# A state-space layer beside a quantized feed-forward on one Trainium2 core: normalization shared with ScalarE, a product two tiles late, parameter loads on another queue, and the last output projection between the scans

## The chip, the core and the metric

The kernel runs on one core of a Trainium2 chip, as one program. The metric is device time in microseconds of a whole execution. Several executions are timed, and one execution is recorded by the profiler.

The engines are named as in the profile: PE is TensorE (matrix products, its weight loads are PEld), DVE is VectorE, ACT is ScalarE, POOL is GpSimd, and SP is the engine that here only starts DMA transfers. Each engine works through its own queue in order. An instruction that has to wait holds everything behind it on its engine. A DMA started by SP or ACT is an instruction of that engine's queue too.

## The reference

The input is x, 8192 tokens of 512 numbers (8 sequences of 1024). Everything is float32.

```python
xn = layernorm(x)                     # mean and variance over the 512, no gain
out = x + mamba(xn) + ffn(xn)

# mamba, DI = 1024 channels, 16 states each
xz = xn @ W_in;  xb, z = split(xz)
xc = silu(causal_conv4(xb) + conv_b)
B, C, dt = split(xc @ W_x);  dt = softplus(dt + dt_bias)      # 16, 16, 1 columns
h_t = h_(t-1) * exp(dt * A) + dt * xc * B                     # A = -exp(A_log)
y = (sum over states of h * C + xc * D) * silu(z)
mamba = y @ W_out

# ffn: every operand is rounded to a 4-bit grid in blocks of 16, each block with its own scale
q = lambda v: grid(v / s) * s,  s = max(abs(block)) / 6
h = silu(q(xn) @ q(w_gate).T) * (q(xn) @ q(w_up).T)           # 1408 columns
ffn = q(h) @ q(w_down).T
```

## The kernel before

The program has four stages.

**Preparation** (`prelude`, class `Job`). There are 52 jobs, each a tile of 128 partitions, most of 1024 numbers: two jobs with the first 512 tokens, twelve with parts of w_gate and w_up, eight with parts of w_down (1024 and 384 numbers in turn), and thirty with the other tokens. A job rounds its tile to the 4-bit grid; a token job also normalizes its tile first. Job 0 and 1, 22 and 23, and so on are pairs of the same chunk of 512 tokens and share their statistics. The steps of a job, with their engines:

- `load` (SP): the tile from DRAM, four buffers.
- `measure` (DVE, L94, L95; ACT, L100): mean and variance for both jobs of a pair, then a square root on ScalarE.
- `deviation` (DVE, L112 to L116): one step of refinement and the reciprocal of the deviation, for both jobs of the pair.
- `normal` (POOL, L124): subtract the mean and multiply, in place, one instruction for each half tile (128 x 512).
- `turn_normal` (PE, ACT, L140): transposes of the normalized tile to PSUM, copies to SBUF, and a store that is issued in the next iteration.
- `scale` (DVE, L154 to L159): the largest absolute value of each block, the scale and its reciprocal, and the tile times the reciprocal. The small values are in PSUM, in the pool whose two buffers later hold the decays of the scans.
- `steps` (ACT, L61, L62): Abs and Exp give the size of the rounding step.
- `round_` (POOL, L167, L168): add that size and subtract it again, which rounds.
- `product` (DVE, L172): times the block's scale.
- `turn_quantized` (PE, ACT, SP): transposes, copies and store of the result.

One iteration of the loop issues parts of several jobs, in the order written there by hand. In iteration i they are: the load of i+3, the stores left by the iteration before, some work of the first scan chunk (its projections, convolution and softplus, one piece for each iteration, `ahead`), `turn_normal(i)`, `deviation(i+1)`, `scale(i)`, `steps(i)`, `normal(i+1)`, `round_(i)`, `measure(i+2)`, `product(i-1)` and `turn_quantized(i-1)`. The order on each engine is the order of issue. Some instructions of the first scans are hoisted into the last third of the loop.

Before that, the constructor starts the loads of the parameters on ScalarE's queue (L239 to L256: W_x, W_out with 2 MB, the convolution weights, three vectors, and A_log in four parts with an Exp behind each, L257).

**Sweep 1 and sweep 2** (`sweep`). The tokens are 16 chunks of 512. Each chunk has 64 pairs of scans: `make_u` (POOL, L638), `make_a` (ACT, L650), the scan itself (DVE, L668), the product with C (DVE, L675, four buffers `hc`), and sums over the states on TensorE (`sum_states`, L685, one group for two pairs). After eight pairs comes a `gate` (DVE, L703, L704), which completes one of the eight slices of y. Other work is put between the pairs: the projections of the next chunk (`ahead`), the output projection of the chunk before (`finish`, L735, and the additions L722), and as `others` the feed-forward (`gate_up` in sweep 1, chunks 0 to 9; `downs` in sweep 2, L894, chunks 10 to 15 of the scans). Side work is paced by planned costs: an estimate of what is left is spread evenly over the slots that are left,

```python
        left = cost + len(now) // per * (29.0 + 64.0 + sums)
        slots = len(now) - TAIL
            credit = min(credit + max(left, 0.0) / max(slots, 1), MOST)
```

where 29 stands for one `finish`, 64 for one `ahead`, and `TAIL` is 12 pairs. The last chunk has no `ahead`.

**End** (in `run`). After the last pair of chunk 15 its sums, its gate and its `finish` are issued: for each of four tiles of 128 tokens eight products of 128x128 by 128x512, which are two instructions each on TensorE, then an addition to what was kept for these tokens, and the store of the output.

Of the kernel before, what the change touches and what calls it, by code (L numbers as in the profile page):

```python
# [17 lines left out]
P = 128  # L18
# [9 lines left out]
T = 512  # L28
# [11 lines left out]
AGAIN = "again"  # L40
TAIL = 12
# [24 lines left out]
class Job:  # L66
# [14 lines left out]
    def measure(self):  # L81

        if not self.pair:
            return
        nc, pp, name = self.nc, self.pp, self.name
        jobs = (self, self.pair)
        n = sum(j.G for j in jobs)
        mv = pp.tile([P, n, 2], F32, tag="mv", name=f"mv_{name}")
        i = 0
        for j in jobs:  # L90
            j.mean, j.at = mv, i
            for g in range(j.G):
                stats = pp.tile([P, 6], F32, tag="stat", name=f"stat_{name}_{i}")
                nc.vector.bn_stats(stats, j.x[:, g * j.W : (g + 1) * j.W])  # L94
                nc.vector.bn_aggr(mv[:, i, :], stats)  # L95
                i += 1
        var = mv[:, :, 1]
        root = pp.tile([P, n], F32, tag="root", name=f"root_{name}")
        rstd = pp.tile([P, n], F32, tag="rstd", name=f"rstd_{name}")
        nc.scalar.activation(root, var, AF.Sqrt, bias=self.net.eps)  # L100
        self.var, self.root, self.r = var, root, rstd
        for j in jobs:
            j.rstd = rstd

    def deviation(self):
        if not self.pair:
            return
        nc, var, root, rstd = self.nc, self.var, self.root, self.r
        n = root.shape[1]

        t = self.net.p_y.tile([P, 2, n], F32, tag="py", name=f"newton_{self.name}")
        nc.vector.reciprocal(t[:, 0, :], root)  # L112
        nc.vector.scalar_tensor_tensor(t[:, 1, :], var, EPS, t[:, 0, :], ALU.add, ALU.mult)
        nc.vector.tensor_tensor(t[:, 1, :], root, t[:, 1, :], ALU.add)
        nc.vector.tensor_scalar(t[:, 1, :], t[:, 1, :], 0.5, None, ALU.mult)
        nc.vector.reciprocal(rstd, t[:, 1, :])  # L116

    def normal(self):
        if self.tokens is None:
            return  # L120
        for g in range(self.G):
            x = self.x[:, g * self.W : (g + 1) * self.W]
            i = self.at + g
            self.nc.gpsimd.tensor_scalar(  # L124
                x, x, self.mean[:, i, 0:1], self.rstd[:, i : i + 1], ALU.subtract, ALU.mult
            )
# [21 lines left out]
    def scale(self):  # L148

        nc = self.nc  # L150
        n = self.K // BLK
        small = self.net.p_a.tile([P, 3, n], F32, tag="ah", name=f"qp_{self.name}")
        top, self.sc, rs = small[:, 0, :], small[:, 1, :], small[:, 2, :]
# [4 lines left out]
        self.v = self.pp.tile([P, self.K], F32, tag="qv", name=f"qv_{self.name}", bufs=3)  # L158
# [19 lines left out]
class Net:  # L178
# [11 lines left out]
    def __init__(self, tc, ctx, x, W_in, conv_w, conv_b, W_x, A_log, D_param, dt_bias, W_out,  # L190
# [46 lines left out]
        nc.vector.memset(self.steep, LEAST)  # L237
        self.Wx = cpool.tile([P, J, self.NS], F32, tag="Wx", name="Wx")
        nc.scalar.dma_start(self.Wx, W_x.rearrange("(j p) n -> p j n", p=P))  # L239
        self.Wout = cpool.tile([P, J, DM], F32, tag="Wout", name="Wout")  # L240
        nc.scalar.dma_start(self.Wout, W_out.rearrange("(j p) m -> p j m", p=P))
        self.cw = cpool.tile([P, J, self.H0 + 1], F32, tag="cw", name="cw")
        nc.scalar.dma_start(self.cw, conv_w.rearrange("(j p) o c -> p j (o c)", p=P))
        vecs = []
        for name, v in (("cb", conv_b), ("dtb", dt_bias), ("Dp", D_param)):
            vt = cpool.tile([P, J], F32, tag=name, name=name)
            nc.scalar.dma_start(vt, v.rearrange("(j p) -> p j", p=P))
# [6 lines left out]
        for s in range(SG):  # L254
            rows = slice(s * D4, (s + 1) * D4)
            nc.scalar.dma_start(A_all[rows], A_log.rearrange("(g d) n -> d g n", d=D4))  # L256
            nc.scalar.activation(  # L257
                self.A[rows],
                A_all[rows].rearrange("d g (q s) -> d g q s", s=SG)[:, :, :, s],
                AF.Exp,  # L260
            )
        nc.vector.tensor_scalar(self.A, self.A, -1.0, -SLOW, ALU.mult, ALU.min)
# [10 lines left out]
        self.Win_v = W_in.rearrange("(k p) n -> p k n", p=P)  # L273
# [41 lines left out]
    def prelude(self, pp):  # L315
# [8 lines left out]
        for i in range(3):  # L324
            part(i, "load")
        part(0, "measure")
# [4 lines left out]
        self.behind = []  # L331
        for i in range(n + 1):
# [13 lines left out]
            part(i, "turn_normal")  # L346
            part(i + 1, "deviation")
            part(i, "scale")
            part(i, "steps")
            part(i + 1, "normal")  # L350
# [5 lines left out]
            part(i - 1, "product")  # L356
            part(i - 1, "turn_quantized")
# [385 lines left out]


# [159 lines left out]
    def run(self):  # L904
# [13 lines left out]
        with ExitStack() as ffn:  # L918
            fp = ffn.enter_context(tc.tile_pool(name="ff", bufs=2))
            with tc.manual_schedule():  # L920
# [3 lines left out]
                self.sweep(pairs, range(SPLIT * per), self.gate_up(fp, range(n)), costs[0])  # L924
        with ExitStack() as ffn:
# [5 lines left out]
            with tc.manual_schedule():  # L931
                self.sweep(
                    pairs, range(SPLIT * per, n * per), self.downs(fp, dT, tiles), costs[1]
                )
                last = self.step[n - 1]
                self.sum_states(last, self.J - 1, NG - 1)
                self.advance()
                self.advance()
                for _ in self.finish(last):
                    self.advance()  # L940
                while self.due:
                    self.advance()
# [5 lines left out]
    def sweep(self, pairs, now, others, cost):  # L948
# [6 lines left out]
        slots = len(now) - TAIL  # L955
        credit = 0.0
        for g in now:
# [54 lines left out]
            if summed and pq < NG - 1:  # L1012
                self.sum_states(self.step[pc], pj, pq)
            self.now += 1
        more = True
# [87 lines left out]
```

## Time and profile before

| | |
|---|---|
| three runs | 5172.91, 5178.5, 5181.34 us (median 5178.5) |
| the profiled execution | 5171.58 us, of which the span of the profile is 5169.7 |
| busy, share of the span | PE 84%, DVE 86%, POOL 78%, ACT 65% |
| preparation | about 0 to 500 us |
| the two sweeps | about 500 to 5135 us, the second from about 3560 |
| end | 5135 to 5169.7 us |

Times in the profile are microseconds from the start of the span. A group of instructions is a line of the source, an engine and an operation with its tiles: its count, busy time and mean duration in ns, then the idle time of the engine just before these instructions and what ended it. A row of the timeline is its start, its duration, engine, line and operation; in brackets stands the idle time before it and the releaser. A wait is a line that waited, an arrow, the line that released it, and the total, the number of times and the longest. A stage's row gives the busy time and the number of instructions of each engine inside it, the granted clock of TensorE as a share of full speed, and the busy share and the rate of the DMA engines.

### The profile page before, as it was taken

How to read it: one execution, taken by the hardware profiler on the slowest of the kernel's cores; microseconds unless marked ns; L12 is line 12 of the kernel's file. 1: busy time of each engine (PE TensorE's matmuls, PEld its weight loads, DVE VectorE, ACT ScalarE, POOL GpSimd, SP SyncE). 2: the span in 40 equal slices, each digit the busy share in tenths (PEclk: the TensorE clock that was granted, in tenths of full speed). 3: DMA queues.
4: the chain of work that ended last, by engine and by line, in shares of the span. 5: the costliest groups of instructions: out<-in, count | busy, mean ns of one | idle time of the engine just before them, and what ended most of it. 6: DMA issues, size and time to landing. Idle time of an engine off the chain costs nothing. (4 is left out here: it accounts for less than half of the span.)

```text
span 5169.7 us, 52154 instructions
## 1 busy us (share of the span) xinstructions
PE 4357.2 (84%) x16324; PEld 2286.0 (44%) x16324; DVE 4463.7 (86%) x4087; ACT 3368.9 (65%) x5037; POOL 4050.4 (78%) x2302
## 2 busy tenths in 40 slices
PE   5535889888898898989898898986999999999975
PEld 2324555554555556455554555551333333333321
DVE  6756888888888988888887898888999999999997
ACT  5655766767667677775767867676656665656543
POOL 5887888878888888887887888887768676767664
PEclk9656999999899999999999999996999999999986
DMA  6665566575656657566575656757686868686852
GB/s 196 198 205 157 143 185 182 155 199 170 180 165 173 192 165 208 143 188 180 162 201 154 191 166 182 200 145 207 178 229 177 239 182 240 175 236 184 228 132 61
DMA packets 582275, 937.45 MB, mean 181 GB/s; under 512 B 53216, under 2 KB 329696, under 8 KB 579824
## 3 DMA queue, kind: packets, MB, share of 16 engines
q1 hardware_dynamic: 571600, 931.61, 64.3%
q10 hardware_dynamic: 10400, 2.52, 0.2%
q8 instruction: 130, 2.13, 0.2%
q14 instruction: 145, 1.19, 0.1%
HBM read 676.76 MB, written 257.20 MB: 181 GB/s over the span
## 5 line engine op out<-in xcount | busy, mean ns | idle before, releaser
L638 POOL TENSOR_TENSOR u<-rep,B 128x1024 f32<-128x1024 f32 x1024 | 2411.3, 2361 | 760.9 <-DVE ah L668 691.6
L650 ACT ACTIVATE ah<-rep,A 128x512 f32<-128x512 f32 x2048 | 1415.8, 692 | 1129.0 <-DVE hc L675 1090.3
L675 DVE TENSOR_TENSOR hc<-ah,C 128x1024 f32<-128x1024 f32 x1024 | 1249.5, 1220 | 77.3 <-PE py L685 35.1
L668 DVE TENSOR_TENSOR_SCAN ah<-ah,state,u 128x1024 f32<-128x1024 f32 x512 | 1199.5, 2343 | 87.0 <-ACT u L656 85.9
L668 DVE TENSOR_TENSOR_SCAN ah<-ah,u 128x1024 f32<-128x1024 f32 x512 | 1169.3, 2284 | 52.3 <-ACT ah L650 46.0
L685 PE MATMUL py<-hc,summed 128*32 128x512 f32 x4096 | 653.5, 635 | 170.9 <-DVE hc L675 119.0
L771 PE MATMUL pu<-wu,xq 128*128 128x256 f32 (+1 forms) x3072 | 693.9, 383 | 101.9 <-ACT hT L824 63.1
L771 PE MATMUL pg<-wg,xq 128*128 128x256 f32 (+1 forms) x3072 | 661.7, 373 | 69.8 <-ACT hT L824 23.3
L771 PEld LDWEIGHTS pu<-wu,xq 128*128 128x128 f32 x3072 | 571.7, 203 | 250.6 <-ACT hT L824 86.7
L894 PE MATMUL pod<-dT,hTr 128*128 128x512 f32 x1408 | 641.7, 606 | 13.3 <-DMA hTr<-hT 9.6
L771 PEld LDWEIGHTS pg<-wg,xq 128*128 128x128 f32 x3072 | 554.0, 195 | 210.3 <-issue 69.5
L498 PE MATMUL pz<-xT,wz 128*128 128x512 f32 x1024 | 506.3, 641 | 69.5 <-ACT h L782 34.8
L437 PE MATMUL px<-xT,wx 128*128 128x512 f32 x1024 | 491.9, 625 | 38.8 <-ACT h L782 21.4
L735 PE MATMUL po<-Wout,y 128*128 128x512 f32 x1024 | 463.8, 604 | 10.7 <-ACT hT L824 4.4
L460 POOL TENSOR_TENSOR xc<-xc,taps 128x509 f32<-128x509 f32 x360 | 413.7, 1149 | 44.3 <-ACT taps L454 25.5
L894 PEld LDWEIGHTS pod<-dT,hTr 128*128 128x128 f32 x1408 | 262.7, 192 | 395.2 <-issue 365.1
L498 PEld LDWEIGHTS pz<-xT,wz 128*128 128x128 f32 x1024 | 204.1, 205 | 338.9 <-issue 232.3
L685 PEld LDWEIGHTS py<-hc,summed 128*32 128x32 f32 x4096 | 91.8, 110 | 564.7 <-DVE hc L675 278.7
L437 PEld LDWEIGHTS px<-xT,wx 128*128 128x128 f32 x1024 | 195.3, 198 | 317.7 <-issue 224.2
L735 PEld LDWEIGHTS po<-Wout,y 128*128 128x128 f32 x1024 | 191.2, 192 | 278.7 <-issue 258.4
L786 DVE TENSOR_TENSOR h<-h,pu 128x512 f32<-128x512 f32 x192 | 121.9, 638 | 179.4 <-PE pu L771 166.3
L650 ACT ACT_TABLE_LOAD x209 | 268.1, 1283 | 3.7
(125 smaller groups left out, 4538.4 us busy)
## 6 DMA issues: line engine op xcount, KB each, us to landing
rep<-ddd SPq DMA_DIRECT2D x512, 512.0 KB, 7.1
ddd<-dd SPq DMA_DIRECT2D x128, 512.0 KB, 3.5
hTr<-hT SPq DMA_DIRECT2D x64, 704.0 KB, 5.8
wg<-gu SPq DMA_DIRECT2D x80, 512.0 KB, 4.9
wu<-gu SPq DMA_DIRECT2D x80, 512.0 KB, 5.9
hT<-hT SPq DMA_DIRECT2D x80, 512.0 KB, 2.9
wx<-in_L_attn_W_in_dram SPq DMA_DIRECT2D x128, 256.0 KB, 3.0
wz<-in_L_attn_W_in_dram SPq DMA_DIRECT2D x128, 256.0 KB, 2.9
```

What stands on the lines that cost most here:

```text
L437: nc.tensor.matmul(px, w[:, k, :], s.xT[:, k, :], start=(k == 0), stop=(k == self.KM - 1))
L460: tt(ca[:, H0 - k :], ca[:, H0 - k :], taps[k][:, : T - H0 + k], ALU.add)
L498: nc.tensor.matmul(b[0], w[:, k, :], s.xT[:, k, :], start=(k == 0), stop=(k == self.KM - 1))
L638: self.nc.gpsimd.tensor_tensor(u, s.reps[j][:, h : h + 2, 1, :], s.B[q].unsqueeze(1).to_broadcast([P, 2, T]), ALU.mult)
L650: nc.scalar.activation(ah[:, i, :], s.reps[j][:, h + i, 0, :], AF.Exp, scale=self.A[:, g, q : q + 1])
L668: nc.vector.tensor_tensor_scan(a, a, u.rearrange("p i t -> p (i t)"), 0.0 if s.first else self.state[:, g, q : q + 1], ALU.mult, ALU.add,)
L675: nc.vector.tensor_tensor(hc, ah, s.C[q].unsqueeze(1).to_broadcast([P, 2, T]), ALU.mult)
L685: nc.tensor.matmul(s.py[i * D4 : (i + 1) * D4, :], self.summed, hcs[i // 2][:, i % 2, :], start=(q == 0), stop=(q == NG - 1),)
L735: nc.tensor.matmul(b[0], s.y[:, j, i * P : (i + 1) * P], self.Wout[:, j, :], start=(j == 0), stop=(j == self.J - 1),)
L771: nc.tensor.matmul(b[0][:, i, :], xq[pair][:, k, i * P : (i + 1) * P], w[:, k, :], start=(k == 0), stop=(k == self.KM - 1),)
L786: nc.vector.tensor_tensor(rows, rows, b[0], ALU.mult)
L894: nc.tensor.matmul(b[0], h[:, k, :], dT[:, k, :], start=(k == 0), stop=(k == self.KF - 1))
```

## The change

Four things are changed.

1. `normal`: the first half of each token tile (the first 128x512) is normalized by ScalarE as an Identity with scale 1/deviation and bias -mean/deviation; GpSimd keeps the second half. `deviation` gets two more small VectorE steps for the bias (`off`).
2. The loop: `product` and `turn_quantized` are those of job i-2, and there is one iteration more. `scale(i)` comes before `deviation(i+1)`, and `normal(i+1)` before `steps(i)`. For the longer lag two jobs share one small tile in PSUM, and `qv` has four buffers.
3. The parameters are loaded by SP, behind the first three tiles (`constants`). The Exps of A_log and the load of W_out follow in iteration 1 (`decays`).
4. Sweep 2 gets a planned cost lower by 64 and ends its side work 7 pairs before the end instead of 12. In the last six pairs `finish_last` puts the first seven of the eight products of tiles 0 to 2 and the first four of tile 3 between the scans; tile 3 uses a buffer of the scans' PSUM pool. After the last gate one product each for three tiles and four for the last remain, each with its addition and store.

The core of the diff:

```diff
 deviation:
         nc.vector.reciprocal(rstd, t[:, 1, :])
+        nc.vector.reciprocal(t[:, 0, :], t[:, 1, :])
+        nc.vector.scalar_tensor_tensor(
+            self.off, self.mean[:, :, 0], -1.0, t[:, 0, :], ALU.mult, ALU.mult
+        )
 normal:
+            if g == 0:
+                self.nc.scalar.activation(
+                    x, x, AF.Identity, bias=self.off[:, i : i + 1], scale=self.rstd[:, i : i + 1]
+                )
+                continue
             self.nc.gpsimd.tensor_scalar(
                 x, x, self.mean[:, i, 0:1], self.rstd[:, i : i + 1], ALU.subtract, ALU.mult
             )
 scale:
-        small = self.net.p_a.tile([P, 3, n], F32, tag="ah", name=f"qp_{self.name}")
+        if not net.small:
+            two = net.p_a.tile([P, 2, 3, P // 2], F32, tag="ah", name=f"qp_{self.name}")
+            net.small = [two[:, i] for i in range(2)]
-        self.v = self.pp.tile([P, self.K], F32, tag="qv", name=f"qv_{self.name}", bufs=3)
+        self.v = self.pp.tile([P, self.K], F32, tag="qv", name=f"qv_{self.name}", bufs=4)
 parameters (constants, called behind the first three loads):
-        nc.scalar.dma_start(...)      # W_x, W_out, conv_w, conv_b, dt_bias, D_param, A_log
+        nc.sync.dma_start(...)        # the same without W_out
+        def decays():
+            nc.sync.dma_start(self.Wout, W_out.rearrange("(j p) m -> p j m", p=P))
+            ...                       # the four Exps of A_log, and A = -exp(A_log)
 prelude:
+        decays = self.constants()
-        for i in range(n + 1):
+        for i in range(n + 2):
             part(i, "turn_normal")
+            part(i, "scale")
             part(i + 1, "deviation")
-            part(i, "scale")
+            part(i + 1, "normal")
             part(i, "steps")
-            part(i + 1, "normal")
+            if i == 1:
+                decays()
             part(i, "round_")
             ...
             part(i + 2, "measure")
-            part(i - 1, "product")
-            part(i - 1, "turn_quantized")
+            part(i - 2, "product")
+            part(i - 2, "turn_quantized")
 sweep (LAST = 6, fp is None in sweep 1; sweep 2 is called with costs[1] - 64.0):
-        slots = len(now) - TAIL
+        slots = len(now) - (TAIL if fp is None else LAST + 1)
+            if fp is not None and g >= len(pairs) - LAST:
+                if ending is None:
+                    while next(others, None) is not None:
+                        assert self.room("other")
+                    ending = self.finish_last(s, fp)
+                if g < len(pairs) - 1:
+                    next(ending)
+        if ending is not None:
+            for _ in range(2):
+                next(ending)
+            self.sum_states(s, self.J - 1, NG - 1)
+            ...                       # the last gate, then the rest of finish_last
+    def finish_last(self, s, fp):
+        ...
+        for i in range(3):
+            banks.append(self.bank([P, self.DM], f"po_{t0 + i}"))
+            matmuls(i, range(4))
+            yield
+            matmuls(i, range(4, J - 1))
+            yield
+        ah = self.p_a.tile([P, 2, T], F32, tag="ah", name=f"po_{t0 + 3}")
+        banks.append([ah[:, 0, :], 3])
+        matmuls(3, range(4))
+        yield
+        for i in range(self.TT):
+            matmuls(i, range(J - 1 if i < 3 else 4, J))
+            nc.vector.tensor_tensor(rs[i], rs[i], banks[i][0], ALU.add)
+            nc.sync.dma_start(self.out[t * P : (t + 1) * P, :], rs[i])
```

## The prediction

> **What bounds the kernel now.** I read the slices of the span first, then busy time by stage, then for each stage the timeline, its waits and its groups, and last the chain that ended last. In the slices I look at the first four columns (129 us each) and the last.
>
> ```profile
> DVE  6756888888888988888887898888999999999997
> ACT  5655766767667677775767867676656665656543
> POOL 5887888878888888887887888887768676767664
> PEclk9656999999899999999999999996999999999986
> ```
>
> The preparation (the first 500 us) is the worst part of VectorE's row. Cut into its stages (us, busy time of PE, PEld, DVE, ACT, POOL, then clock, DMA share, GB/s):
>
> ```profile
> 44.50:106.80 62.30, 43.76 (x132) 21.83 (x132) 51.03 (x77) 38.60 (x51) 38.30 (x18) 0.89 0.63 217
> 106.80:171.30 64.50, 41.15 (x122) 20.03 (x121) 46.46 (x92) 40.55 (x58) 35.38 (x23) 0.81 0.56 184
> ...
> 205.00:345.00 140.00, 54.40 (x239) 44.20 (x239) 99.36 (x191) 101.49 (x130) 135.16 (x69) 0.57 0.63 208
> ...
> 5020.00:5137.00 117.00, 53.50 (x128) 5.45 (x128) 112.56 (x70) 51.46 (x98) 65.87 (x29) 0.50 0.27 63
> ```
>
> The first two are the weight jobs: no engine is full, VectorE is nearest. The third is the token jobs: GpSimd is full (135 of 140). The last is the end of the scans: VectorE full, TensorE at half clock. Start of the run, timeline:
>
> ```profile
> 4.30 7.27 ACTq L247 DMA_DIRECT2D cb<-in_L_attn_conv_b_dram  x1
> ...
> 17.38 1.28 ACT L257 ACT_TABLE_LOAD   x1 [17.38 <-DMA Dp<-in_L_attn_D_param_dram]
> ...
> 21.31 0.30 ACT L100 ACTIVATE root_x<-mv_x,eps 128x4 f32<-128x4 f32 x1
> ...
> 26.92 1.23 DVE L154 TENSOR_REDUCE qp_x<-wt_x 128x64 f32<-128x1024 f32 x1 [3.32 <-POOL wt_x L124]
> ```
>
> ScalarE issues the parameter loads one after another until 17 us, and the first square root stands behind them, although the statistics were ready at 8.96. From 106.8 to 171.3, in the weight jobs, the longest of VectorE's waits (total, times, longest) shows the product one tile behind the rounding:
>
> ```profile
> DVE qv_d L172 <- POOL qv_d L168: 6.8, 3, 4.2
> ```
>
> Groups of the token stage, 205 to 345:
>
> ```profile
> L124 POOL TENSOR_SCALAR wt_x<-wt_x,mv_x,rstd_x 128x512 f32<-128x512 f32 x31 | 64.1, 2076 | 0.0
> L167 POOL TENSOR_TENSOR qv_x<-qv_x,qm_x 128x1024 f32<-128x1024 f32 x15 | 32.0, 2130 | 3.7 <-ACT qm_x L62 3.7
> L168 POOL TENSOR_TENSOR qv_x<-qv_x,qm_x 128x1024 f32<-128x1024 f32 x15 | 31.9, 2128 | 1.2
> ```
>
> GpSimd has hardly any idle time (after the bar), and in the same answer VectorE's L154 waits 31.5 us for the normalization L124. The chain at the end:
>
> ```profile
> 5135.42 1.92 PE py L685 x4
> 5137.35 28.58 PE po L735 x64
> ```
>
> After the last scan 64 matmuls stand bare on the path.
>
> **The change part by part.** The sum is made against the profiled execution, 5171.6 us (span 5169.7); the median of the three runs is 6.9 us higher, and I carry that difference over.
>
> Start. Without parameter loads ahead of it, the square root can run at 9.1. Then 0.30, seven small VectorE steps (five took 0.92, two more of 0.17: 1.25), and GpSimd's half, 2.08 with 0.1 of signalling: the first L154 at 13.0 instead of 26.92, 13.9 earlier. The loads now stand on SP's queue, their issue times there adding to 16 us (0.49, 2.37, 7.27, 3.05, 0.59 and 2.3 for A_log), ahead of the fourth tile's load. That one issues near 19 and lands near 23 (median landing of such a load 3.9); its L154 ran at 43.28, so would be at 29.4: hidden with 6 us to spare. The 2 MB load of W_out now goes out at the second tile; behind it on SP's queue stand the sixth tile's load and the store that the first projection needs. At the 400 GB/s that the DMA showed at 10 us it holds them 5 us, inside the 13.9. Decays: four ACTIVATEs of 0.42 and one VectorE step behind them, under 2 us once. I take 13; bounds 5 (the SP issues take twice as long) and 15.
>
> The Trainium skill (DMA: Bandwidth & Descriptors, "Issuing engines are not separate DMA queues") says that the queue a transfer is started from only matters for the sequencer's time to start it, usually small beside the transfer. Here the 4 KB load of cb held ScalarE's queue for 7.27 us, and the measurement decides; by the page this edit would be worth about nothing and the time 13 us longer.
>
> Weight jobs, 44.5 to 171.3. The product two tiles late no longer waits for the rounding: VectorE's waits for L168 in the two stretches are 1.9, 3.3 and 6.8, 12.0 together. Next is VectorE itself (97.5 busy of 126.8), then its waits for ScalarE's convolution rows, 11.1, which I leave. I take 12; bounds 4 and 20.
>
> Token jobs, 171.3 to 456, 284.7 us for 30 jobs: 30 periods of 8.41 (two L124 of 2.08 and L167, L168 of 2.13), 10.0 of GpSimd's L582, and 19.2 in which VectorE stood (358.9 to 378.1) while the first fetches for the scans held the load queue. Afterwards per job GpSimd has 2.08 + 4.26 = 6.34. ScalarE per pair of jobs: 8 copies 4.28, Abs and Exp 4.42, two new Identities priced by L443, the same form from PSUM (0.77), one root 0.30, two table loads 2.57: 13.1, or 6.55 per job. VectorE per pair: two scalings (L154 to L159, 3.66), two products of 1.20, statistics 3.2, the longer deviation 1.25: 14.2. On ScalarE, Abs and Exp of the tile before are queued behind the Identity that waits for the deviation, and GpSimd's rounding waits for them; with the product two tiles later that has a period to spare. On VectorE the deviation stands one product before the scaling that needs it, and GpSimd's half takes 2.08: 0.95 of wait, so 15.1 per pair or 7.56 per job. VectorE is what is late next. 30 x 7.56 = 227; the four softplus steps now meet a tighter ScalarE (1.33 + 2.57 each, half of it shown: 8); L582 fits into GpSimd's slack; the fetch stall stays, 19. Together 254: 30 saved. Bounds: 5, if ScalarE's order keeps the period at 8.41 (279.5), and 53, if neither the wait nor the softplus shows (7.09 per job and 19).
>
> The extra iteration of the loop holds one product, copies and stores that existed before: nothing. The shared small tile frees both jobs' scales two products later, and VectorE is in order past them by then: nothing.
>
> Sweep 2. The estimate that paces the side work falls by 64, and its slots grow by 5: 3.57 per pair instead of 3.79. TensorE was 0.95 busy from 3750 to 5000, VectorE 0.95, against 0.96 alone at the end, so relief can give at most 1% of 1250, 13 us; the same work filling the free end can cost that much. I take 4; bounds -8 and 13.
>
> End. From the last gate but one (y at 5113.94) to the end of the span are 55.8 us. Afterwards TensorE does sums (1.93), 50 matmuls of 0.43 (25 of the 32 products, two each) with four at 0.85 on the cold clock (the row: about 2 us at half clock from 5137.3), and three sums of 1.06: done at 28.3, later than the last scan's 21.5. Sums wait behind projections in TensorE's queue, but the four hc buffers keep VectorE going. Then gate 1.5, 14 matmuls 6.0, one addition 0.8, the store 3.1: 39.7. Saved 16; bounds 8 (half clock throughout the first ten microseconds and again behind the gate) and 22 (warm throughout).
>
> The Trainium skill (TensorE: Matmul & The Clock Gate, "What's actually happening") speaks against this place: after an idle window of 3.4 us work starts at half clock until a busy one has passed. By the page up to 3.4 us start cold instead of about 2, an estimate of 0.7 us lost.
>
> Sum: 13 + 12 + 30 + 4 + 16 = 75. 5171.6 - 75 = 5096.6 for a profiled run, 5103.5 by the median.
>
> **The rivals.** ScalarE becomes the bound of the token stage: it has the least slack (13.1 of 15.1) and its Abs and Exp now stand behind an Identity that waits for the deviation; the waits L167 <- L62 (3.7) speak for it, the two-tile lag against. The stage then gains 5 instead of 30: 5128.5.
>
> Everything hides better: weights 20, tokens 48, sweep 13, end 18, start 14 = 113: 5065.5. For it speaks that VectorE's rows overlap by 0.1 each; against it, that some wait always comes up.
>
> Slower: the same Identity closes a loop per job instead of being slack: deviation 1.25, Identity 0.77, Abs 1.06, table load 1.28, Exp 1.15, GpSimd 2.08 + 4.26 = 11.85 per job. 30 jobs and 27 are 383, 98 more than now; less the 45 of the other parts, 53 slower: 5231.5. It decides from 10.1 us per job (284.7 + 45 - 27 over 30). For it: between 177 and 207 the period was 9.7 to 9.9 with GpSimd waiting for Exp. Against it: the product no longer asks for the same tile.
>
> That it does not do what it says (scheduling moves the root back behind other work, TensorE stays cold): start and token parts zero, 12 + 4 + 8 gives 5154.5, still faster.
>
> **How the numbers follow.** About 0.2% is what a measurement tells from no change (10 us). Forecast 0.62, with a range of its own from 5085 to 5122; ScalarE-bound 0.19; hides better 0.10; does not do what it says 0.04; slower 0.03; cancelled to within 0.2% 0.02. Faster is 0.62 + 0.19 + 0.10 + 0.04 = 0.95, same 0.02, slower 0.03. The range reaches to the ScalarE case above and halfway to the better one: 5080 to 5134.
>
> **What would show it.** First L154 near 13; no wait of products for rounding; token rounds every 7.6 us with GpSimd near 0.84 busy; 25 projections between the last scans and 14 matmuls after the last gate. Wrong if token rounds stay above 8.2, if the fourth tile's load is waited for, or if VectorE waits for TensorE in the last six pairs.

## The result, and the profile after

The changed kernel takes 5138.04 us (median of four runs, 5133.51 to 5139.24) beside 5176.74 for the kernel before on the same chip: a ratio of 0.9927, with a 95% interval from 0.9913 to 0.994. It is 38.7 us faster. The forecast was 75 us less, or 5103.5; the measured time lies 34.5 us above that and 4 above the top of the stated range. The profiled execution took 5139.24 us, its span is 5137.4.

Lines have moved in the changed file: the first line of the scaling is L168 (L154 before), GpSimd's normalization L135 (L124), ScalarE's new half L131, rounding L181 and L182 (L167, L168), the product L186 (L172), Abs and Exp L62 and L63, copies of transposed tiles L151, convolution rows of the first chunk L508 (ScalarE) and L517 (VectorE), softplus L607 and the product behind it L612, the last projections L784.

In the slices of the page, VectorE's first four columns rise from 6756 to 7767, and GpSimd is no longer near full in the second and third:

```profile
DVE  7767888887888988888887898888999999999998
ACT  5866676857668677775767767676656665665543
POOL 5676888888888888887887888787777776767654
PEclk9657999999999999989999999996999999999999
```

By stage (us, busy time of PE, PEld, DVE, ACT, POOL, clock, DMA share, GB/s; the same pieces of work as the four rows of before, except that the last begins at the last gate but one):

```profile
31.00:93.28 62.28, 41.62 (x131) 21.15 (x130) 50.42 (x76) 38.51 (x51) 38.34 (x19) 0.92 0.64 220
93.28:156.20 62.92, 42.70 (x131) 21.61 (x130) 47.01 (x95) 41.60 (x60) 33.32 (x21) 0.86 0.57 187
190.00:330.00 140.00, 59.25 (x258) 48.99 (x259) 104.30 (x214) 113.39 (x151) 110.73 (x56) 0.55 0.65 213
5096.00:5137.00 41.00, 34.89 (x96) 13.18 (x96) 26.19 (x20) 8.19 (x15) 7.86 (x4) 0.92 0.18 64
```

The weight jobs (rows one and two) take 125.2 us where they took 126.8: hardly less, and still no engine is full. In the token jobs (row three) GpSimd fell from 135 to 111 of 140, but nothing else is full either: VectorE 104, ScalarE 113. So waits, not an engine, set the pace there. In the end (row four) TensorE is now busy.

Start, timeline:

```profile
4.62 3.24 SPq L268 DMA_DIRECT2D cb<-in_L_attn_conv_b_dram  x1
...
7.78 0.30 ACT L102 ACTIVATE root_x<-mv_x,eps 128x4 f32<-128x4 f32 x1 [5.76 <-DVE mv_x L97]
...
11.33 1.23 DVE L168 TENSOR_REDUCE qp_x<-wt_x 128x64 f32<-128x1024 f32 x1 [1.95 <-POOL wt_x L135]
```

The root no longer stands behind parameter loads; the first scaling runs 15.6 us earlier. The load of cb, which held ScalarE's queue for 7.27 us, now holds SP's for 3.24, and all the parameter loads together held SP's queue until 12.19 us.

VectorE's waits in the weight jobs, first after (31 to 156), then the row of before that the prediction told of but did not show (44.5 to 171.3):

```profile
DVE xc L517 <- ACT over L508: 21.5, 6, 6.6
DVE qp_x L168 <- POOL wt_x L135: 1.5, 1, 1.5
```

```profile
DVE xc L487 <- ACT over L478: 11.0, 6, 3.4
```

The 12.0 us in which products waited for rounding are gone, as forecast. But the wait for ScalarE's convolution rows grew by 10.5. The longest of the six places in the timeline:

```profile
33.17 1.21 DVE L186 TENSOR_TENSOR qv_x<-qv_x,qp_x 128x1024 f32<-128x1024 f32 x1
...
36.75 5.51 PE L467 MATMUL px<-xT,wx 128*128 128x512 f32 x8 [4.94 <-DMA wx<-in_L_attn_W_in_dram]
...
42.10 1.04 PE L150 MATMUL ptq_x<-ident,qv_x 128*128 128x128 f32 x8
...
42.74 1.07 ACT L151 COPY stq_x<-ptq_x 128x512 f32<-128x512 f32 x2 [7.15 <-PE ptq_x L150]
...
44.37 0.27 ACT L508 ACTIVATE over<-px,cw 128x3 f32<-128x3 f32 x1
...
44.68 1.53 DVE L517 SCALAR_TENSOR_TENSOR xc<-px,cw,xc 128x509 f32<-128x509 f32 x2 [6.57 <-ACT over L508]
```

The product is done at 34.38. Its transposes stand in TensorE's queue behind a projection (L467), which itself waited for its weights; ScalarE's copies wait for the transposes, and the convolution row stands behind the copies.

Waits in the token jobs after, 156.2 to 434:

```profile
DVE qp_x L168 <- POOL wt_x L135: 41.6, 22, 4.9
...
POOL qv_x L181 <- ACT qm_x L63: 47.6, 19, 4.0
...
ACT stn_x L151 <- DMA xnT<-stn_x: 24.5, 8, 6.0
```

VectorE still waits 41.6 us for GpSimd's half (51.2 before), though GpSimd has time to spare. GpSimd itself now waits 47.6 us for Exp (6.4 before). One place in the timeline shows the chain; in brackets stands the idle time before a row and its releaser:

```profile
299.38 1.33 ACT L607 ACTIVATE dd<-row,dtb 128x512 f32<-128x512 f32 x2
...
304.79 1.15 ACT L63 ACTIVATE qm_x<-qm_x,steep 128x1024 bf16<-128x1024 bf16 x1
...
306.02 2.12 POOL L181 TENSOR_TENSOR qv_x<-qv_x,qm_x 128x1024 f32<-128x1024 f32 x1 [2.43 <-ACT qm_x L63]
308.22 2.14 POOL L182 TENSOR_TENSOR qv_x<-qv_x,qm_x 128x1024 f32<-128x1024 f32 x1
310.31 2.51 POOL L612 TENSOR_TENSOR dd<-dd,xc 128x512 f32<-128x512 f32 x2
312.79 2.09 POOL L135 TENSOR_SCALAR wt_x<-wt_x,mv_x,rstd_x 128x512 f32<-128x512 f32 x1
314.91 1.23 DVE L168 TENSOR_REDUCE qp_x<-wt_x 128x64 f32<-128x1024 f32 x1 [4.92 <-POOL wt_x L135]
```

Softplus (L607) delays Exp on ScalarE; rounding waits for Exp; GpSimd's half of a later tile stands in GpSimd's queue behind that rounding and behind L612; and the scaling of that later tile waits 4.92 us. It is a loop over two tiles: scaling of i, Abs and Exp of i, rounding of i, GpSimd's half of i+2, scaling of i+2. A pair of jobs with neither softplus nor the scans' fetches in it (a quiet pair below) takes 15.64 us near the end of the stage; the others (disturbed pairs) take up to 20.9, and the one with the fetches 38.9.

End, timeline of TensorE:

```profile
5099.09 7.92 PE L784 MATMUL po<-Wout,y 128*128 128x512 f32 x14
...
5107.94 6.28 PE L784 MATMUL po<-Wout,y 128*128 128x512 f32 x14
...
5115.14 9.71 PE L784 MATMUL po<-Wout,y 128*128 128x512 f32 x22
...
5127.45 6.28 PE L784 MATMUL po<-Wout,y 128*128 128x512 f32 x14 [1.60 <-DVE y L734]
```

50 matmuls now run before the last gate (the last scan's own work on VectorE ends at 5118.52, so most of the 22 run behind it) and 14 behind the gate.

### The profile page after: what moved, and what is told of

Its sections match the earlier page's. It is cut to its first block, busy times and chain, and to the rows that moved or that the text cites. A ratio compares the mean times of both kernels' runs of the same rounds, so it can differ in the third digit from the quotient of the medians.

```text
span 5137.4 us, 52165 instructions
## 1 busy us (share of the span) xinstructions
PE 4360.9 (85%) x16324; PEld 2294.4 (45%) x16324; DVE 4468.1 (87%) x4119; ACT 3385.0 (66%) x5068; POOL 3985.9 (78%) x2270
## 5 line engine op out<-in xcount | busy, mean ns | idle before, releaser
L715 PE MATMUL py<-hc,summed 128*32 128x512 f32 x4096 | 631.0, 624 | 136.9 <-DVE hc L705 91.8
L955 PE MATMUL pod<-dT,hTr 128*128 128x512 f32 x1408 | 653.4, 614 | 39.4 <-DMA hTr<-hT 26.9
L467 PE MATMUL px<-xT,wx 128*128 128x512 f32 x1024 | 498.9, 632 | 40.5 <-ACT h L843 21.4
L765 PE MATMUL po<-Wout,y 128*128 128x512 f32 x960 | 438.5, 608 | 12.4 <-ACT hT L885 4.4
L467 PEld LDWEIGHTS px<-xT,wx 128*128 128x128 f32 x1024 | 198.0, 201 | 326.9 <-issue 236.5
L765 PEld LDWEIGHTS po<-Wout,y 128*128 128x128 f32 x960 | 179.9, 193 | 265.5 <-issue 247.5
L847 DVE TENSOR_TENSOR h<-h,pu 128x512 f32<-128x512 f32 x192 | 121.9, 638 | 181.1 <-PE pu L832 149.5
```

The source lines that it names most:

```text
L467: nc.tensor.matmul(px, w[:, k, :], s.xT[:, k, :], start=(k == 0), stop=(k == self.KM - 1))
L715: nc.tensor.matmul(s.py[i * D4 : (i + 1) * D4, :], self.summed, hcs[i // 2][:, i % 2, :], start=(q == 0), stop=(q == NG - 1),)
L765: nc.tensor.matmul(b[0], s.y[:, j, i * P : (i + 1) * P], self.Wout[:, j, :], start=(j == 0), stop=(j == self.J - 1),)
L847: nc.vector.tensor_tensor(rows, rows, b[0], ALU.mult)
L955: nc.tensor.matmul(b[0], h[:, k, :], dT[:, k, :], start=(k == 0), stop=(k == self.KF - 1))
```

## The experiments

Twelve kernels ran, in three comparisons of four, each beside its own runs of the kernel before (5166.18, 5170.74 and 5178.93 us). The table cuts each profiled span at the same events: the start of the third job's scaling; that of job 22's; that of job 51's; the first gate; the first gate of chunk 10; the last gate but one; the end. All in us, each within 0.1 of the trace, so that a row adds up to its span. The runs of one comparison (e1 to e4, e5 to e8, e9 to e12) shared a chip.

| kernel | ratio to before (95%) | start | weights | tokens | to first gate | sweep 1 | chunks 10 to 15 | end |
|---|---|---|---|---|---|---|---|---|
| before | | 38.5 | 132.5 | 280.6 | 72.5 | 3114.1 | 1474.2 | 57.2 |
| after | 0.9927 (0.9913, 0.994) | 25.0 | 129.9 | 268.7 | 73.4 | 3121.4 | 1477.1 | 41.8 |
| e1 preparation alone | 0.9958 (0.9943, 0.9972) | 25.0 | 131.1 | 269.2 | 73.7 | 3114.5 | 1474.3 | 57.2 |
| e2 sweep 2 and end alone | 0.9975 (0.9966, 0.9984) | 38.4 | 132.9 | 280.1 | 72.3 | 3110.4 | 1476.9 | 40.8 |
| e3 lag of one tile | 0.9945 (0.9929, 0.9962) | 26.1 | 131.0 | 268.8 | 74.9 | 3111.0 | 1479.9 | 42.2 |
| e4 rounding later | 0.9915 (0.99, 0.993) | 25.0 | 129.1 | 255.2 | 73.8 | 3114.0 | 1479.4 | 42.4 |
| e5 the change again | 0.9931 (0.9916, 0.9946) | 25.0 | 130.4 | 268.5 | 73.3 | 3114.8 | 1479.7 | 42.3 |
| e6 additions later | 0.9916 (0.9901, 0.9931) | 25.0 | 121.8 | 268.4 | 73.3 | 3111.0 | 1479.4 | 42.2 |
| e7 four buffers | 0.9924 (0.9908, 0.9941) | 25.0 | 131.9 | 264.8 | 70.0 | 3105.3 | 1482.4 | 40.8 |
| e8 planned cost as before | 0.9936 (0.9919, 0.9953) | 24.9 | 129.3 | 268.8 | 73.3 | 3111.2 | 1480.5 | 41.8 |
| e9 GpSimd normalizes all | 0.9959 (0.9944, 0.9974) | 27.0 | 133.3 | 285.0 | 72.1 | 3120.5 | 1470.6 | 42.2 |
| e10 e4, e6, e7 together | 0.9859 (0.9844, 0.9874) | 25.1 | 122.6 | 244.7 | 71.1 | 3123.4 | 1474.0 | 42.3 |
| e11 and fetches spread | 0.9816 (0.9799, 0.9834) | 25.0 | 121.9 | 229.4 | 71.0 | 3128.7 | 1479.3 | 40.8 |
| e12 pacing all as before | 0.992 (0.9905, 0.9935) | 25.0 | 130.1 | 270.0 | 71.9 | 3121.5 | 1477.3 | 41.9 |

**e1_prep: the preparation alone.**

```diff
-                    costs[1] - 64.0, fp,
+                    costs[1], None
                 )
+                last = self.step[n - 1]
...
+                for _ in self.finish(last):
+                    self.advance()
```

> The whole preparation of the change with the sweeps and the end of before. In the profile of the change the first gate of the scans came 27.2 us earlier than before, but at the end of sweep 1 only 19.8 us were left. Theory A: the preparation is worth 27 (half of the 55 that were forecast), and what sweep 1 gave back is drift of the granted clock that another execution need not show: 5147 to 5153 us, first gate again near 497. Theory B: sweep 1 answers to the earlier start and always gives 7 back: 5155 to 5158. By the forecast (13 + 12 + 30): 5122.

Measured: 5145.44 against 5166.18 us, 20.7 us less. Up to the first gate the profile is 25.2 us ahead of before; sweep 1 took 3114.5. Theory A holds: the preparation keeps what it gains.

**e2_end: sweep 2 and the end alone.** The hunks of the change in the sweep, `finish_last` and `run`, on the kernel before.

> The preparation of before with the pacing and the end of the change. Theory A: sweep 2 and end together gain 12 to 13 us, because the feed-forward products that used to be done by 5001 us now run into the last chunk, so that part of the 16 us saved at the end is paid for there: 5163 to 5166 us. By the forecast (4 + 16): 5157. If sweep 1 alone loses 7 us from the other start (theory B of the first kernel), sweep 1 is here as long as before, about 3114 us from the first gate to that of chunk 10.

Measured: 5152.68 us, 13.5 less. The end fell by 16.4, chunks 10 to 15 rose by 2.7: what theory A said, with less given back. Both parts together would be 34.2, about what the change shows on this level (e5: 37.0), so no interaction is seen that is clear of the intervals.

**e3_lag1: the lag undone.**

```diff
-            part(i - 2, "product")
-            part(i - 2, "turn_quantized")
+            part(i - 1, "product")
+            part(i - 1, "turn_quantized")
```

> The change with the product and the transposes of the rounded tile one tile late again. Theory A: the lag is worth next to nothing in the weight jobs, because VectorE's wait for the rounding (12.0 us before) only became a longer wait for ScalarE's convolution rows (11.0 us before, 21.5 in the change): with one tile the waits come back on L186 and go from L517, and the rounds of jobs 2 to 21 span 125 to 128 us as in the change (125.2) and before (126.8). In the quiet token pairs the product would be ready at the moment it is issued (rounding ends at 405.87, product at 405.94), so the pair stays near 15.7; total 5138 to 5148. By the forecast the lag is worth 12 in the weight jobs alone: 5150 or more.

Measured: weights 131.0, tokens 268.8, both as in the change. VectorE's waits in the weight jobs (31 to 156) are those of before again:

```profile
DVE xc L517 <- ACT over L508: 11.5, 5, 3.5
DVE qv_d L186 <- POOL qv_d L182: 7.1, 3, 4.4
DVE qv_u L186 <- POOL qv_u L182: 3.4, 1, 3.4
DVE qv_g L186 <- POOL qv_g L182: 2.1, 1, 2.1
```

12.6 us stand at the product and 11.5 at the convolution, where the change has 0 and 21.5. The lag moves a wait from one line to the other. In this form it is worth nothing, in either stage.

**e4_round_late: rounding one tile later.**

```diff
-            part(i, "round_")
+            part(i - 1, "round_")
```

> The change with GpSimd's rounding one tile later, so that GpSimd normalizes its half of tile i+2 before it rounds tile i. Theory A: the token stage is held by a loop over two tiles: scaling of i, Abs and Exp on ScalarE, rounding of i, GpSimd's half of i+2, scaling of i+2; any delay of ScalarE (softplus, a copy that waits for a store) goes through it to VectorE, which waits 41.6 us for L135. With the rounding one tile later these waits fall below 15, a quiet pair takes 14.2 to 14.6 instead of 15.64, and the token stage loses 20 to 28 us: 5110 to 5120. Theory B: ScalarE itself is too full in the disturbed pairs (18 to 20 us): only the quiet pairs gain, 1 us each for six pairs: 5130 to 5136.

Measured: tokens 255.2, 13.5 less than the change; quiet pairs took 14.78 us (rounds at 373.30 and 388.08) instead of 15.64. VectorE's waits from 190 to 320:

```profile
DVE qp_x L168 <- ACT wt_x L131: 10.2, 7, 2.9
...
DVE qp_x L168 <- POOL wt_x L135: 2.6, 3, 0.9
```

In the corresponding stretch of the change (190 to 330) the wait for L135 was 27.9. So the loop over two tiles is the mechanism. Theory A's 20 to 28 was too much: what ScalarE loses in the disturbed pairs now reaches VectorE through ScalarE's own half (L131). With the rounding one tile late, a product one tile late would stand right behind its own rounding; the edit was made with the product two tiles late only, and without that lag it was not run.

**e5_again: the change once more.**

> The changed kernel once more, beside the others of this comparison. Theory A (sweep 1 drifts from execution to execution): sweep 1, from the first gate to that of chunk 10, takes 3110 to 3116 us instead of the 3121.4 of the first profile; first gate near 497 to 500 again; sweep 2 and the end 1518 to 1522. The time is 0.9927 of before again, 37 to 40 us less.

Measured: 5133.78 us, 37.0 less; sweep 1 took 3114.8 with the same code that showed 3121.4. As theory A said, the first profile's 7 us there belong to that execution and not to the code.

**e6_adds_late: the convolution additions behind the product.**

```diff
             part(i, "round_")
-            for work in self.behind:
-                work()
-            self.behind = []
             part(i + 2, "measure")
             part(i - 2, "product")
             part(i - 2, "turn_quantized")
+            for work in self.behind:
+                work()
+            self.behind = []
```

> The change with VectorE's convolution additions (L517) moved behind the product and its transposes of the same iteration. Theory A: in the weight jobs VectorE stands 21.5 us for ScalarE's convolution rows, which stand in ScalarE's queue behind the copies of the tile before; one product of 1.2 us and the earlier transposes fit into each of the eight waits: the stage from the third scaling to job 22's falls from 129.9 to 118 to 122 us, 8 to 12 us less in all. Theory B: ScalarE's queue (copies that wait for TensorE, then the row) sets the period, and the wait only moves to another line: within 3 us of the change.

Measured: weights 121.8, 8.1 less than the change; the wait fell to 13.5 (31 to 148):

```profile
DVE xc L517 <- ACT over L508: 13.5, 4, 6.2
```

Theory A holds: the wait that took the place of the product's was on the path. It fell by 8.0 us, and the stage by 8.1.

**e7_st4: four buffers for transposed tiles.**

```diff
-        st = self.pp.tile([P, kn, self.G, P], F32, tag="st", name=...)
+        st = net.pool.tile([P, kn, self.G, P], F32, tag="hc", name=..., bufs=4)
```

> The change with four buffers instead of two for the transposed tiles (stn, stq), in a tile of the scans that is free during the preparation, so that ScalarE's copies don't wait for stores. In the token stage ScalarE waited 24.5 us for stores in 8 places (longest 6.0), in the disturbed pairs. Theory A: these waits pass through Exp, rounding and GpSimd's half to VectorE: the token stage (scaling of job 22 to that of job 51) falls from 268.7 by 8 to 15 us. Theory B: the softplus steps set the disturbed pairs and ScalarE catches up by the next one: less than 4 us.

Measured: tokens 264.8, 3.7 less than e5, and 3.3 less on the way to the first gate. ScalarE's waits for stores in the token jobs are gone from the list, and yet theory B is nearer: most of the 24.5 us were not on the path by themselves.

**e8_pace: the planned cost as before.**

```diff
-                    costs[1] - 64.0, fp,
+                    costs[1], fp,
```

> The change with the planned cost of sweep 2 not lowered by 64, the end as in the change. Theory A: with the lowered cost the last chunk, from its first gate to its last but one, took 188.0 us in all four profiles with it and 184.2 to 184.6 in the two without, and chunks 10 to 14 took 1289 to 1292 either way; so undoing it gives 184 to 185 and 3 to 4 us less in all. Theory B: the projections now put between the last pairs are what lengthens the last chunk: 188 again and no difference. By the forecast the lowered cost is worth 4 us, which would be lost: 192 or a longer chunk 10 to 14.

Measured: the last chunk fell to 185.3 us as in theory A, but chunks 10 to 14 rose to 1295.2 from 1291.6 (e5). Together 1480.5 against 1479.7: nothing is saved. Theory A was right on the last chunk. Whether the 3.6 us in chunks 10 to 14 are its counterpart is not shown: with the lowered cost these chunks took from 1282.5 (e9) to 1294.4 (e7).

**e9_poolnorm: GpSimd normalizes both halves.**

```diff
-            if g == 0:
-                self.nc.scalar.activation(
-                    x, x, AF.Identity, bias=..., scale=...
-                )
-                continue
```

> The change with both halves of a token tile normalized by GpSimd again; the lag, the order and the parameter loads as in the change. Theory A: since the lag alone is worth nothing, all of the 12 us that the token stage gained come from ScalarE's half; GpSimd is full again (two normalizations of 2.08 and rounding of 4.26: 8.41 per job), and the stage from the scaling of job 22 to that of job 51 takes 278 to 284 us instead of 268.5, 10 to 15 us more in all. Theory B: the lag and the new order carry the token stage, and without ScalarE's half it stays below 274.

Measured: tokens 285.0, 16.5 more than e5 and 4.4 more than before. GpSimd is full again (190 to 330):

```profile
190.00:330.00 140.00, 59.58 (x253) 47.34 (x251) 95.35 (x194) 99.95 (x127) 131.69 (x67) 0.55 0.63 204
```

ScalarE's half carries all the gain of the token stage, and more: the rest of the change costs this stage 4.4, for a reason that no run here isolates. The start of 27.0 against 25.0 puts 2.0 us of the start's gain down to ScalarE's half too.

**e10_best: e4, e6 and e7 together**, with a third buffer for qm.

> Three of the single edits together: the rounding one tile later (13.4 us in the token stage), the convolution additions behind the product (8.5 in the weight stage), four buffers for transposed tiles (3.7, and 3 behind it), and a third buffer for qm. Theory A: they act at different places and add up: the weight stage 120 to 123 us, the token stage 248 to 253, 24 to 28 us less than the change. Theory B: with the rounding late, ScalarE sets the token stage and the stores hold ScalarE, so that the buffers are worth more together (245 or less).

Measured: 5106.42 against 5178.93 us. Weights 122.6, tokens 244.7: 23.8 less than e5 in the tokens, where the single edits add up to 17.0. Theory B was right on the size. Its reason fits e4, where ScalarE waited 20.1 us for stores in the token jobs (155 to 410) and no longer does here. But the third buffer for qm was not run alone, so its part is not shown; e4, with two such buffers, has no wait of Abs (L62) for GpSimd, which speaks against a large one.

**e11_spread: the first fetches of the scans, two per iteration.**

```diff
-                self.later(2, lambda: self.fetch_first(s))
+                for n_, f in enumerate(self.fetches_first(s)):
+                    self.later(2 + n_ // 2, f)
```

> The same with the first fetches of the scans spread over six iterations of the token jobs instead of one. In the change SP issues 32 small fetches and four large ones from 326.5 to 344, and the next tile's load stands behind them in SP's queue: VectorE waits 21.0 us for it. Theory A: it is SP's queue; with at most eight issues between two loads the wait falls below 6 and the token stage by another 12 to 18 us. Theory B: it is the 4 MB that they move; spread out they slow the other loads and stores instead, and ScalarE and GpSimd stand at the first scans' instructions until the last fetch lands: less than 5 us.

Measured: 5088.19 us against 5178.93, the fastest of all kernels here. Tokens 229.4, 15.3 less than e10. VectorE's waits from 147 to 395 in e10, then in this kernel:

```profile
DVE stat_x L96 <- DMA wt_x<-in_L_attn_x_dram: 25.1, 4, 22.1
```

```profile
DVE stat_x L96 <- DMA wt_x<-in_L_attn_x_dram: 5.4, 4, 1.9
```

The gain has the size of theory A; its cause is shown only in part. Here is the stall of e10 (309.97 to 332.08), cut where SP issued the load:

```profile
309.97:319.35 9.38, 0.00 (x0) 0.00 (x0) 0.00 (x1) 1.69 (x2) 5.23 (x3) 0.52 0.52 138
319.35:332.08 12.73, 0.00 (x0) 0.00 (x0) 0.00 (x0) 0.82 (x2) 0.77 (x1) 0.50 1.03 236
```

For 9.4 us the load had not been issued, which is SP's queue. For another 12.7 it had been issued and had not landed, where the median of such loads in the kernel before was 3.9; the DMA engines were full then (share 1.03), which is the bytes of the fetches. The edit spreads both, issues and bytes, and also puts the large fetches first, so the run does not tell their parts of the 15.3 us. Theory B's price, less than 5 us to gain, did not hold.

**e12_slots: all of sweep 2's pacing as before, the end as in the change.**

```diff
-        slots = len(now) - (TAIL if fp is None else LAST + 1)
+        slots = len(now) - TAIL
```

and `costs[1]` as in e8.

> The change with the side work of sweep 2 paced exactly as before (cost not lowered, ending 12 pairs before the end), the end as in the change. From the first gate of chunk 10 to the last but one of chunk 15 the two kernels with the pacing of before took 1474.2 and 1474.3 us, the six with the change's 1476.9 to 1480.5. Theory A: it is the side work in the last chunk that lengthens it; paced as before the stretch takes 1474 again, the feed-forward products end near 5000 on the scale of before, and 4 to 6 us are saved. Theory B: the stretch differs by the granted clock or by chance: 1477 to 1480 again.

Measured: chunks 10 to 15 took 1477.3 us, and the gain is not there. With e9 (1470.6) and e10 (1474.0), which have the pacing of the change, theory B is what remains: the stretch scatters from 1470.6 to 1482.4, and the pacing cannot be told from no change. Only the last chunk (first gate to last but one) follows the pacing: 184.6 here, 185.3 in e8 and 184.2 and 184.6 in before and e1, against 188.0 to 188.4 in the ten profiles with the pacing of the change.

## Why the prediction was right in direction and wrong in two terms

The direction held, and so did the mechanisms of the start, of the end and of ScalarE's half. The time of 5138.04 lies outside the stated range, 5080 to 5134: the terms of the weight jobs (9.4 us missing) and of the token jobs (18.1) carry most of the miss, sweep 2's term 6.9. Term by term, measured by the table's cuts on the first pair of profiles:

- **Start: 13 forecast, 13.5 measured.** The agreement is partly luck, two errors that nearly cancel. The first scaling came at 11.33 instead of 13.0, since the root could run at 7.78. What was taken for under 2 us, the decays, was more: VectorE stood 4.61 us for the Exps of A_log ahead of L298, and L298 took another 1.77. The parameter loads held SP's queue for 9.9 us (2.25 to 12.19), not 16, and the fourth tile's load was issued at 12.24, not near 19; it was not waited for, and its scaling ran at 29.64 (29.4 forecast). By the Trainium skill's remark on issuing queues (DMA: Bandwidth & Descriptors, "Issuing engines are not separate DMA queues") moving the loads would be worth about nothing; the start gained 13.5 us, 2.0 of them by ScalarE's half (e9), and no run moves the loads alone.
- **Weight jobs: 12 forecast, 2.6 measured (132.5 to 129.9).** The step that failed is "then its waits for ScalarE's convolution rows, 11.1, which I leave". They were next, and not constant: 11.0 became 21.5. A row is computed by ScalarE behind the copies of the tile before. At three of the six places (6.57, 3.54 and 1.91 us of the 21.5) these copies waited for transposes that stood behind a projection in TensorE's queue; at the other three (3.15, 3.70 and 2.65) ScalarE was busy with silu and Exp, each behind a table load of 1.28. At none was the product what was missing. So the row came no earlier, while VectorE, no longer held at the product, reached the additions earlier. e3 and e6 show it from both sides. The working priced what is removed, and compared the remainder with VectorE's busy time, not with the next wait on the same engine. The 2.6 itself is about the size of the scatter: with the same weight stage the profiles of after, e1, e5, e7, e8 and e12 take 129.3 to 131.9.
- **Token jobs: 30 forecast, 11.9 measured (280.6 to 268.7).** The 29 periods between the two cuts would be 29 x 7.56 + 8 + 19 = 246.2 by the forecast's rates; against the 280.6 of before that is 34.4 less, more than the 30, because the forecast's rates for before (29 x 8.41 + 10.0 + 19.2 = 273.1) leave 7.5 of the 280.6 out. Measured are 29 x 7.82 (the quiet pair of 15.64 us) = 226.8, 21.0 of fetch stall, and 20.9 in the disturbed pairs: 7.5, 2.0 and 12.9 more than forecast. Without the stall that is 8.54 us per job, over the 8.2 that the prediction named as the sign of being wrong. The step that failed is "with the product two tiles later that has a period to spare". Only the product has it. GpSimd's half of tile i+2 is queued behind the rounding of tile i, which waits for Exp, and the scaling of i+2 waits for that half. In quiet pairs this adds a second wait of 0.83 (one of 0.95 was counted, 0.81 and 0.83 came). In disturbed ones it passes softplus on, and L612 too, which "fits into GpSimd's slack" only if nobody waits behind it. e4 cuts the loop and gains 13.5. The rival with ScalarE as the bound had the right lines in it (Abs and Exp behind Identity, rounding waiting for Exp) but too small a gain, 5 instead of 12, and ScalarE was not full (113 of 140); the slower rival's loop was sought within one tile and lies over two, where it doesn't lengthen the period beyond the old one.
- **Sweep 1: nothing forecast, and nothing shown.** The first profile lost 7.3 us; e1, e3, e4 and e5, with the preparation of the change or nearly that, took 3111 to 3115, like before.
- **Sweep 2's pacing: 4 forecast; nothing measurable.** The first pair shows 2.9 us more, e8 and e12 don't bring it back, and the stretch scatters by 11.8 from run to run.
- **End: 16 forecast, 15.4 measured.** TensorE was done with the last sums 28.7 us after the last gate but one (28.3 forecast). The first 14 matmuls took 7.92 us at a granted clock of 0.79 (5099.1 to 5107.0), and the same number took 6.28 at 1.00: 1.64 lost, where 1.7 was counted. The four cold matmuls of the forecast are 3.4 us of half clock and not the 2 of the row beside them, and half clock lasted until 5102.4, 3.3 us into these 14; so the 0.7 us that the forecast thought it might lose here was in its sum already. VectorE waited 7.40 us for TensorE at the last gate; the forecast had it so, with 28.3 against the last scan's 21.5.

Terms of the sum with their measures: 13.5 + 2.6 + 11.9 - 0.9 (way to the first gate) - 2.9 + 15.4 = 39.6, less the 7.3 of sweep 1 in that one profile: 32.3, which is the difference of the two profiled runs (5171.58 and 5139.24). The medians differ by 38.7: the profiled run of before was 5.2 us faster than its median, that of the change 1.2 slower than its own.

## What to carry to other kernels

When a wait is taken away, look for the next wait of the same engine in the same stretch and ask whether it is measured from a point that now moves; do not compare with the engine's busy time. When work is split between engines in a software pipeline, write down the loop through every queue over as many tiles as the lag reaches: here one instruction's place in GpSimd's queue tied two tiles together, and moving the rounding by one tile was worth 13.5 us where the split itself was worth 16.5. A run of transfers in front of a load on the issuing queue delays it twice, by the time to issue them (9.4 us in e10) and by the time to move their bytes (12.7 us to landing instead of 3.9); spreading the run over iterations took 15 us.

## What the runs showed of the hardware that was not expected

L298 (128x128, 0.23 us before) took 1.77 us in the change and 1.76 or 1.77 in the eleven other profiles with that start:

```profile
22.86 2.12 POOL L181 TENSOR_TENSOR qv_x<-qv_x,qm_x 128x1024 f32<-128x1024 f32 x1
23.30 1.77 DVE L298 TENSOR_SCALAR A<-A 128x128 f32<-128x128 f32 x1 [4.61 <-ACT A L293]
```

and before:

```profile
22.75 2.08 POOL L124 TENSOR_SCALAR wt_x<-wt_x,mv_x,rstd_x 128x512 f32<-128x512 f32 x1 [21.45 <-DVE rstd_x L116]
...
23.37 0.23 DVE L262 TENSOR_SCALAR A<-A 128x128 f32<-128x128 f32 x1 [0.73 <-ACT A L257]
```

L298 began at 23.30 and ended at 25.07, and GpSimd's rounding L181, with two tensor operands, ran from 22.86 to 24.98. In the kernel before the same instruction ran beside GpSimd's normalization L124, with one tensor operand, and was not slowed. The Trainium skill (SBUF — State Buffer, "SBUF: two separate sides") says that VectorE in some modes and GpSimd exclude each other from a shared port pair for a whole instruction; the first case agrees with that, the second shows a GpSimd instruction that did not shut VectorE out. No run here changes one of the two instructions alone, and none shows in which mode VectorE ran.

Sweep 1 has the same instructions in the same order in all fourteen profiles, and took 3105 to 3115 us in e1 to e8 and 3120 to 3129 in e9 to e12, where the kernel before was slower too (5178.93 against 5166.18 and 5170.74). A difference of 10 us in one pair of profiles says nothing of a change; the same cut in several kernels does.
